# Macaron block on one core: the last feed-forward's tokens turned by VectorE and DMAs instead of TensorE

## The chip, the core and the metric

The kernel runs on one core of a Trainium2 chip. The metric is the device time of one execution in microseconds (us). A core has five engines that run side by side, each with its own instruction stream in order: TensorE (PE in the profile, with its weight loads as PEld), VectorE (DVE), ScalarE (ACT), GpSimd (POOL) and SyncE (SP, which here issues DMAs). They wait for each other by semaphores.

## The reference

The input is 16 sequences of 256 tokens with 256 features, all float32. The block is two half-weighted feed-forwards around an attention:

```python
x = x + 0.5 * ffn(layernorm(x), w1, b1, w2, b2)
x = x + attn(layernorm(x), Wq, Wk, Wv, Wo)      # 16 heads, rotary, causal
x = x + 0.5 * ffn(layernorm(x), w1, b1, w2, b2)

def ffn(x, w1, b1, w2, b2):                     # 256 -> 1024 -> 256
    h = gelu(x @ ternary(w1).T + b1)
    return h @ ternary(w2).T + b2
```

`ternary` rounds the weights to -1, 0 and 1 by a threshold. The layer norm has no gain and no bias.

## The kernel before

All 4096 tokens stay in SBUF, as eight tiles `xs[i]` of 128 partitions x 4 x 256 (a block of 512 tokens: `BT = 4` tiles of 128 tokens). The kernel runs the first feed-forward (`ffn(0, ...)`), the attention sequence by sequence (`slot`), and the last feed-forward (`ffn(2, store)`), with some overlap where they meet.

A feed-forward is a loop of steps `u`; a step has a block `i` and an eighth `f` of the 1024 hidden features. `up(i, f)` multiplies the transposed, normalized tokens `xnT[i]` with 128 columns of `w1q` into a PSUM tile named `m` (two buffers). `xnT` has two parts, a rounded `high` and the `rest`, both float32r, so that `up` is four matmuls of 128x512. ACT then computes the gelu twice from PSUM, once rounded (`h_high`) and once in full (`h_whole`), and the difference of both, `h_rest`, is made on DVE, or on POOL for f = 1, 3 and 5. `down(i, f)` runs `LATE = 2` steps later and adds the products with `w2q` into a PSUM tile `w`: eight matmuls of 128x256, alternating between `h_high` and `h_rest`. After the eighth, two DVE instructions add half the result to `xs[i]`, and `store` issues two DMAs of 256 KB on SP.

The next block's input is prepared on the way. In `step`, at f = 4 to 7 DVE computes the statistics of block i + 2 (`stats`: `st`, `mv`), and POOL makes `rstd` from them (`finish_stats`: `var`, then a power). At f = 3 `prepare(i + 1)` lets DVE normalize the four token tiles into `xn` (one buffer). At f = 5 and 6 `turn_in(i + 1, k)` turns one half of the features: PE transposes four 128x128 pieces into a PSUM tile `mm`, ACT copies them to `high`, and DVE subtracts to get `rest`. At f = 6 `add_bias(i)` adds the output bias on POOL.

The order on each engine is the order of the program for everything that is issued through the `InOrder` wrappers `tensor`, `vector`, `scalar`, `gpsimd` and `sync`. The stores go through the plain `nc.sync`, and the scheduler places them. Almost every instruction has the wrapper's line (L196) in the profile, so it is told apart by the names of its tiles.

Of the kernel before, what the change touches and what calls it, by code (L numbers as in the profile page):

```python
# [8 lines left out]
FP = mybir.dt.float32  # L9
FR = mybir.dt.float32r  # L10
BF = mybir.dt.bfloat16
AF = mybir.ActivationFunctionType
ALU = mybir.AluOpType
# [3 lines left out]
P = 128  # L17
D = 256
KC = D // P
FF = 1024  # L20
NFC = FF // P
# [9 lines left out]
def kernel(  # L31
# [17 lines left out]
    BT = 4  # L49
    TB = BT * P  # L50
    NBLK = NT // TB
# [3 lines left out]
    small = ctx.enter_context(tc.tile_pool(name="small", bufs=4))  # L55
    fp = ctx.enter_context(tc.tile_pool(name="ffn", bufs=2))
# [19 lines left out]
    b1_sb = const.tile([P, NFC], FP, name="b1_sb")  # L76
    b2_sb = const.tile([P, D], FP, name="b2_sb")
    cos_sb = const.tile([P, 2, HD], FP, name="cos_sb")
    sin_sb = const.tile([P, 2, HD], FP, name="sin_sb")
    xs = [state.tile([P, BT, D], FP, name=f"x_{i}") for i in range(NBLK)]  # L80

    flat1, flat2 = (state.tile([P, 2 * FF], FP, name=f"w_{n}") for n in range(2))
# [19 lines left out]
    for k in range(KC):  # L102
        rows = slice(k * P, (k + 1) * P)
        nc.sync.dma_start(out=wv[:, k, :], in_=wqkvT[rows, 2 * D :])
        for at in range(0, 2 * D, 4 * HD):
            n, j, e = at // D, at // P % 2, at // (4 * HD) % 2
            nc.sync.dma_start(
                out=wqk[:, k, n, j, :, e, :],
                in_=wqkvT[rows, at : at + 4 * HD].rearrange("p (r d) -> p r d", d=HD),
            )  # L110
    for at in range(0, P, HD):
        r, n = at // 32, at // HD % 2
        nc.sync.dma_start(
            out=wo[at : at + HD, :, :],
            in_=woT.rearrange("(k n r d) f -> n r d k f", n=2, r=4, d=HD)[n, r],
# [19 lines left out]
        out=mask_k,  # L135
        in_=mask_k,
# [10 lines left out]
        out=mask_b,  # L147
        in_=mask_b,
# [9 lines left out]
        out=ident_b,  # L158
        in_=ident_b,
# [25 lines left out]
    mv = [state.tile([P, NTILE, 2], FP, name=f"mv_{i}") for i in range(3)]  # L185
    rstd = [state.tile([P, NTILE], FP, name=f"rstd_{i}") for i in range(3)]
# [17 lines left out]
    def tokens(n):  # L204
        return xs[n // BT][:, n % BT, :]

    def stats(ln, n):
        st = small.tile([P, 6], FP, name="st")
        vector.bn_stats(st, tokens(n))
        vector.bn_aggr(mv[ln][:, n, :], st)  # L210

    def finish_stats(ln, first, n):

        var = small.tile([P, BT], FP, name="var")
        gpsimd.tensor_scalar(
            var[:, 0:n], mv[ln][:, first : first + n, 1], LN_EPS, 1.0, ALU.add, ALU.mult
        )
        gpsimd.tensor_tensor(
            rstd[ln][:, first : first + n], var[:, 0:n], power[:, 0:n], ALU.pow
        )  # L220
# [78 lines left out]

    LATE = 2  # L300

    def ffn(ln, after):
        xn, xnT, hT, ys = {}, {}, {}, {}

        def measure(i):
            if ln == 0:
                for t in range(BT):
                    stats(0, i * BT + t)
                finish_stats(0, i * BT, BT)

        def prepare(i, engine=None):
            xn[i] = fp.tile([P, BT, D], FP, name="xn", bufs=1)
            for t in range(BT):
                normalize(ln, i * BT + t, xn[i][:, t, :], engine)
            xnT[i] = [fp.tile([P, KC, TB], FR, name=f"xnT_{n}") for n in range(2)]

        def add_bias(i):
            gpsimd.tensor_add(xs[i], xs[i], b2_sb.unsqueeze(1).to_broadcast([P, BT, D]))

        def turn_in(i, k):  # L320
            tp = ps_mm.tile([P, TB], FP, name="mm")
            for t in range(BT):
                tensor.transpose(
                    tp[:, t * P : (t + 1) * P], xn[i][:, t, k * P : (k + 1) * P], ident
                )
            high, rest = (xnT[i][n][:, k, :] for n in range(2))
            scalar.copy(high, tp)
            return lambda: vector.tensor_sub(rest, tp, high.bitcast(FP))

        first = {}  # L330

        def up_first(i, f, to=None):
            h = first[i, f] = ps_m.tile([P, TB], FP, name="m") if to is None else to
            for n in range(2):
                for k in range(KC):
                    tensor.matmul(
                        h,
                        w1q[:, k, f * P : (f + 1) * P],
                        xnT[i][n][:, k, :],
                        start=(n == 0 and k == 0),  # L340
                        stop=(n == 1 and k == KC - 1),
                    )

        def up(i, f):
            if (i, f) not in first:
                up_first(i, f)
            h = first.pop((i, f))
            high = fp.tile([P, TB], FR, name="h_high", bufs=LATE + 3)
            rest = fp.tile([P, TB], FR, name="h_rest", bufs=LATE + 3)
            whole = fp.tile([P, TB], FP, name="h_whole", bufs=3)  # L350
            scalar.activation(high, h, AF.Gelu, bias=b1_sb[:, f : f + 1])
            scalar.activation(whole, h, AF.Gelu, bias=b1_sb[:, f : f + 1])

            engine = gpsimd if f in (1, 3, 5) and not (ln == 0 and i == NBLK - 1) else vector
            engine.tensor_sub(rest, whole, high.bitcast(FP))
            hT[i, f] = (high, rest)

        def down(i, f):
            if f == 0 and ln == 2 and i == NBLK - 1:

                ys[i] = [ps_mm.tile([P, 2, D], FP, name="mm") for t in range(0, BT, 2)]
            elif f == 0:
                y = ps_w.tile([P, BT, D], FP, name="w")
                ys[i] = [y[:, t : t + 2, :] for t in range(0, BT, 2)]
            parts = hT.pop((i, f))
            order = [(t, n) for t in range(BT) for n in range(2)]
            if ln == 2 and (i, f) == (NBLK - 1, NFC - 1):

                order = [(t, n) for n in range(2) for t in range(BT)]
            for t, n in order:  # L370

                tensor.matmul(
                    ys[i][t // 2][:, t % 2, :],
                    parts[n][:, t * P : (t + 1) * P],
                    w2q[:, f, :],
                    start=(f == 0 and n == 0 and t % 2 == 0),
                    stop=(f == NFC - 1 and n == 1 and t % 2 == 1),
                )
            if f == NFC - 1:
                for t in range(0, BT, 2):  # L380
                    xt = xs[i][:, t : t + 2, :]
                    vector.scalar_tensor_tensor(
                        xt, ys[i][t // 2], 0.5, xt, ALU.mult, ALU.add
                    )
                for t in range(0, BT, 2):
                    after(i, t)

        def begin():
            measure(0)
            if ln == 0:  # L390
                sizes(0)
            prepare(0)
            if ln == 0:
                threshold(0)
                signs(0, lambda w: w[:, :, 0 : FF // 2])
            for k in range(KC):
                turn_in(0, k)()
            if ln == 0:
                signs(0, lambda w: w[:, :, FF // 2 :])
                sizes(1)  # L400

        def step(u):
            i, f = divmod(u, NFC)
            if i < NBLK:
                up(i, f)
                if ln == 0 and u == 0:
                    threshold(1)
                if ln == 0 and u in (0, 3):
                    part = slice(0, NFC // 2) if u == 0 else slice(NFC // 2, NFC)
                    signs(1, lambda w: w[:, part, :])  # L410
                if ln == 0 and u == 4:
                    gpsimd.tensor_scalar(b2_sb, b2_sb, 0.5, 0.0, ALU.mult, ALU.add)
                if u == 1:
                    measure(1)
                if i + 1 < NBLK and (ln, i) != (2, 0):
                    if f == 3:
                        prepare(i + 1)
                    if f in (5, 6):
                        turn_in(i + 1, f - 5)()
                if f >= 4 and i + 2 < NBLK:  # L420
                    stats(ln, (i + 2) * BT + f - 4)
                    if f == NFC - 1:
                        finish_stats(ln, (i + 2) * BT, BT)
                if f == (1 if i == NBLK - 1 else 6):
                    add_bias(i)
            if u >= LATE:
                down(*divmod(u - LATE, NFC))
            if ln == 0 and u == 2 * NFC + 2:
                make_tables()
            if ln == 0 and u < (NBLK - 1) * NFC and later:  # L430
                later.pop(0)()

        return begin, step, prepare, turn_in, up_first
# [353 lines left out]
    rest = []  # L787
# [96 lines left out]
```

## Time and profile before

| | us |
|---|---|
| median of 3 runs | 600.56 (599.93 to 601.11) |
| profiled execution, its own time | 599.31 |
| its span | 597.5 |
| PE busy | 580.0 (97%) |
| DVE busy | 473.5 (79%) |
| ACT busy | 391.1 (65%) |
| POOL busy | 324.8 (54%) |

The granted TensorE clock is 1.00 of full speed over the span. The last feed-forward takes about the last 130 us: from its first steps at about 465 us to the end it has 48 transposes of `xn` on PE (272 ns each by their rows, which overlap), 24 normalizations on DVE (408 ns), 62 rounded and 62 full gelus from `m` on ACT (688 and 681 ns), and DMAs moved 1 to 59 GB/s in stretches of 20 us.

How to read the rows that follow: `out<-in` are the names of the tiles, then partitions x elements and the type; `x4` is the number of instructions that are merged into a row. The chain of work that ended last is followed back from the last instruction, at each step to what released it. Times of PE in the chain are the spacing of its instructions, since matmuls are pipelined.

### The profile page before, as it was taken

What the parts mean: (1) busy time and instruction counts of PE and PEld (TensorE: products, weight loads), DVE (VectorE), ACT (ScalarE), POOL (GpSimd) and SP (SyncE); (2) the same over time, 40 slices, a digit from 0 to 9 for tenths busy, and PEclk for the clock granted to TensorE, in tenths of its full rate; (3) what the DMA queues carried; (4) which work ended last, traced back from release to release, by engine and by line L of the source; (5) the groups of instructions that cost most, each with busy time, mean ns of one, the idle gap of its engine ahead of it and who ended that gap; (6) DMA issues with size and microseconds to landing.
All of it is one profiled execution on the core that took longest, in us unless ns stands there. A gap on an engine that the chain in (4) does not pass through costs nothing.

```text
span 597.5 us, 14414 instructions
## 1 busy us (share of the span) xinstructions
PE 580.0 (97%) x5398; PEld 467.2 (78%) x5398; DVE 473.5 (79%) x1690; ACT 391.1 (65%) x668; POOL 324.8 (54%) x301
## 2 busy tenths in 40 slices
PE   4999999999999999999999999999999999999996
PEld 3798989887777777777777777777767788888886
DVE  6877888677688999899899999999986466666743
ACT  4576666675476666766667676676765666666664
POOL 4645665693555576555855668464821454455452
PEclk9999999999999999999999999999999999999999
DMA  8810000000010011100110001100000011111101
GB/s 282 196 27 2 1 1 1 36 1 19 19 39 20 20 38 37 37 23 20 38 38 28 31 19 38 38 20 28 31 4 2 2 36 36 36 36 36 35 30 41
DMA packets 25588, 21.26 MB, mean 36 GB/s; under 512 B 11056, under 2 KB 21168, under 8 KB 25520
## 3 DMA queue, kind: packets, MB, share of 16 engines
q1 hardware_dynamic: 24960, 19.44, 10.3%
q8 instruction: 42, 0.69, 0.5%
q10 hardware_dynamic: 560, 0.92, 0.4%
q14 instruction: 26, 0.21, 0.1%
HBM read 7.51 MB, written 4.19 MB: 20 GB/s over the span
## 4 chain that ended last, share of the span: by engine, by line
PE 88%; DVE 5%; ACT 3%; issue 1%; DMA 1%; POOL 1%; DVEq 0%; SPq 0%; POOLq 0%; ACTq 0%
PE mm L196 35%; PE w L196 31%; PE m L196 23%; DMA w<-in_w1T_dram 1%; DVE xn L196 1%; ACT h_high L196 1%; DVE masked L196 1%; ACT h_whole L196 1%; DVE w2q L196 1%; DVE h_rest L196 1%; DVE w L196 1%; DVE st L196 0%; POOL h_rest L196 0%; DVE x L196 0%; ACT pT L196 0%
## 5 line engine op out<-in xcount | busy, mean ns | idle before, releaser
L196 DVE CUSTOM_DVE_ANT_0 masked<-m,mask_q 128x128 f32<-128x128 f32 x480 | 142.1, 351 | 20.6 <-PE m L196 19.7
L196 PE MATMUL m<-xnT,w1q 128*128 128x512 f32 x504 | 143.3, 405 | 0.9 <-ACT xnT L196 0.7
L196 ACT ACTIVATE pT<-w 128x768 f32<-128x768 f32 x128 | 104.1, 814 | 56.3 <-DVE w L196 55.9
L196 ACT ACTIVATE h_high<-m,b_sb 128x512 fp32r<-128x512 f32 x126 | 86.7, 688 | 79.4 <-PE m L196 79.3
L196 DVE TENSOR_TENSOR h_rest<-h_whole,h_high 128x512 fp32r<-128x512 f32 x83 | 74.7, 900 | 60.3 <-ACT h_whole L196 59.9
L196 PE MATMUL w<-w2q,h_high 128*128 128x256 f32 x480 | 120.7, 285 | 0.3 <-DVE w2q L196 0.3
L196 PE MATMUL w<-qT,kT 32*128 32x256 f32 (+1 forms) x1024 | 120.5, 348 | 0.0
L196 PE MATMUL w<-w2q,h_rest 128*128 128x256 f32 x480 | 118.0, 279 | 0.8 <-POOL h_rest L196 0.7
L196 PEld LDWEIGHTS w<-qT,kT 32*128 32x128 f32 x1024 | 90.3, 184 | 33.6 <-issue 22.8
L196 PE MATMUL m<-kT,qT 32*128 32x128 f32 x960 | 115.0, 349 | 0.3 <-ACT kT L196 0.3
L196 POOL TENSOR_TENSOR h_rest<-h_whole,h_high 128x512 fp32r<-128x512 f32 x45 | 60.1, 1335 | 85.3 <-ACT h_whole L196 85.1
L196 PEld LDWEIGHTS m<-xnT,w1q 128*128 128x128 f32 x504 | 87.4, 191 | 16.4 <-DVE xnT L196 2.9
L196 PEld LDWEIGHTS w<-w2q,h_rest 128*128 128x128 f32 x480 | 90.4, 188 | 5.9 <-POOL h_rest L196 1.2
L196 PEld LDWEIGHTS w<-w2q,h_high 128*128 128x128 f32 x480 | 90.3, 188 | 5.0 <-DVE w2q L196 0.8
L196 DVE TENSOR_TENSOR w<-w,mask_k 128x512 f32<-128x512 f32 x123 | 85.5, 695 | 3.7 <-PE w L196 3.6
L196 ACT ACTIVATE h_whole<-m,b_sb 128x512 f32<-128x512 f32 x126 | 85.8, 681 | 0.0
L196 POOL TENSOR_TENSOR o<-avs,inv 128x256 f32<-128x256 f32 x32 | 20.3, 635 | 91.6 <-DVE inv L196 91.6
L196 PE MATMUL mm<-xnT_a,wqk 128*128 128x256 f32 x256 | 68.5, 392 | 0.0
L196 PEld LDWEIGHTS m<-kT,qT 32*128 32x128 f32 x960 | 66.2, 185 | 1.5 <-ACT kT L196 0.7
L196 POOL TENSOR_TENSOR w<-w,cosT 128x512 f32<-128x512 f32 x32 | 41.3, 1289 | 27.0 <-ACT kT L196 13.4
L196 PEld LDWEIGHTS mm<-xnT_a,wqk 128*128 128x128 f32 x256 | 45.8, 189 | 10.0 <-issue 1.3
L196 POOL TENSOR_TENSOR w<-w,sinT 128x512 f32<-128x512 f32 x32 | 40.9, 1277 | 20.4 <-DMA w<-w 20.4
(92 smaller groups left out, 885.8 us busy)
## 6 DMA issues: line engine op xcount, KB each, us to landing
w<-w SPq DMA_DIRECT2D x64, 128.0 KB
out_dram<-x SPq DMA_DIRECT2D x15, 256.0 KB
x<-in_x_dram SPq DMA_DIRECT2D x7, 512.0 KB
w<-in_w2T_dram SPq DMA_DIRECT2D x1, 1024.0 KB
qT<-mT SPq DMA_DIRECT2D x64, 4.0 KB
w<-in_w1T_dram SPq DMA_DIRECT2D x1, 512.0 KB
w<-in_w1T_dram ACTq DMA_DIRECT2D x1, 512.0 KB
wqk<-in_wqkvT_dram SPq DMA_DIRECT2D x16, 32.0 KB
```

The source lines that it names most:

```text
L196: return tc.keep_in_program_order(getattr(self.engine, name)(*args, **kwargs))
```

## The change

It concerns the last feed-forward alone, and its blocks 3 to 7 (`by_blocks`). Blocks 0 to 2 are prepared as before.

- The statistics of such a block are computed at f = 2 and 3, two blocks ahead, and at f = 6 DVE makes an `offset`, minus mean times `rstd`.
- ACT normalizes the four token tiles at f = 6 and 7, as an activation with `rstd` as scale and the offset as bias.
- At f = 0 of the next block, DVE transposes the tile by blocks of 32x32 into `turned`, the second half of a weight buffer that is free by then. One DMA writes it to a DRAM tile `rows` (512 KB), and four DMAs of 128 KB bring its rows, in runs of 128 elements, into the `rest` part of `xnT`. All five are issued by SP.
- `turn_in` then only copies to `high` on ACT, and DVE subtracts in place.
- The tokens of such a block stand in another order (four groups of 32 in turn), so the gelus read and write permuted views, which puts the order right.
- The output bias of blocks 1 to 6 is added in two halves, at f = 2 and 4 instead of f = 6.

```diff
+    turned = flat2[:, FF:]
+    dram = ctx.enter_context(
+        tc.tile_pool(name="rows", bufs=2, space=bass.MemoryType.DRAM)
+    )
     def ffn(ln, after):
+        by_blocks = range(3, NBLK if ln == 2 else 0)
...
+        def offsets(i):
+            offset[i] = small.tile([P, BT], FP, name="offset", bufs=2)
+            of = slice(i * BT, (i + 1) * BT)
+            vector.scalar_tensor_tensor(
+                offset[i], mv[ln][:, of, 0], -1.0, rstd[ln][:, of], ALU.mult, ALU.mult
+            )
+        def normalize_by_blocks(i, t0, t1):
...
+                scalar.activation(
+                    xn[i][:, t, :],
+                    tokens(n),
+                    AF.Identity,
+                    bias=offset[i][:, t : t + 1],
+                    scale=rstd[ln][:, n : n + 1],
+                )
+        def turn_by_blocks(i):
+            vector.transpose(turned, xn[i].rearrange("p n (j t) -> p j n t", t=32))
+            rows = dram.tile([P, 2 * TB], FP, name="rows")
+            sync.dma_start(out=rows, in_=turned)
+            of = rows.rearrange("(a f) (k j q) -> j f k a q", a=4, k=KC, j=4)
+            xnT[i] = [fp.tile([P, KC, TB], FR, name=f"xnT_{n}") for n in range(2)]
+            for j in range(4):
+                sync.dma_start(
+                    out=xnT[i][1][32 * j : 32 * j + 32]
+                    .bitcast(FP)
+                    .rearrange("p k (a q) -> p k a q", a=4),
+                    in_=of[j],
+                )
-        def add_bias(i):
-            gpsimd.tensor_add(xs[i], xs[i], b2_sb.unsqueeze(1).to_broadcast([P, BT, D]))
+        def add_bias(i, t0=0, t1=BT):
+            xt = xs[i][:, t0:t1, :]
+            gpsimd.tensor_add(xt, xt, b2_sb.unsqueeze(1).to_broadcast([P, t1 - t0, D]))
         def turn_in(i, k):
+            if i in by_blocks:
+                high, rest = (xnT[i][n][:, k, :] for n in range(2))
+                scalar.copy(high, rest.bitcast(FP))
+                return lambda: vector.tensor_sub(rest, rest.bitcast(FP), high.bitcast(FP))
...
-            scalar.activation(high, h, AF.Gelu, bias=b1_sb[:, f : f + 1])
-            scalar.activation(whole, h, AF.Gelu, bias=b1_sb[:, f : f + 1])
+            for to in (high, whole):
+                if i in by_blocks:
+                    to = to.rearrange("p (n a t) -> p a n t", n=BT, a=4)
+                    of = h.rearrange("p (a n t) -> p a n t", n=BT, a=4)
+                else:
+                    of = h
+                scalar.activation(to, of, AF.Gelu, bias=b1_sb[:, f : f + 1])
...
         def step(u):
             i, f = divmod(u, NFC)
+            if f == 0 and i > 0 and i + 1 in by_blocks:
+                turn_by_blocks(i + 1)
...
-                    if f == 3:
+                    if f == 3 and i + 1 not in by_blocks:
                         prepare(i + 1)
                     if f in (5, 6):
                         turn_in(i + 1, f - 5)()
-                if f >= 4 and i + 2 < NBLK:
-                    stats(ln, (i + 2) * BT + f - 4)
-                    if f == NFC - 1:
-                        finish_stats(ln, (i + 2) * BT, BT)
-                if f == (1 if i == NBLK - 1 else 6):
+                if i + 2 < NBLK:
+                    early = i + 2 in by_blocks
+                    for at in {2: (0, 1), 3: (2, 3)}.get(f, ()) if early else (f - 4,):
+                        if at >= 0:
+                            stats(ln, (i + 2) * BT + at)
+                        if at == BT - 1:
+                            finish_stats(ln, (i + 2) * BT, BT)
+                    if early and f == 6:
+                        offsets(i + 2)
+                    if early and f in (6, 7):
+                        normalize_by_blocks(i + 2, 2 * (f - 6), 2 * (f - 5))
+                if ln == 2 and 0 < i < NBLK - 1:
+                    if f in (2, 4):
+                        add_bias(i, f - 2, f)
+                elif f == (1 if i == NBLK - 1 else 6):
                     add_bias(i)
```

More of the change, by code (lines that the diff above doesn't have):

```diff
@@ L315, in prepare @@
             xnT[i] = [fp.tile([P, KC, TB], FR, name=f"xnT_{n}") for n in range(2)]
-        def add_bias(i):
-            gpsimd.tensor_add(xs[i], xs[i], b2_sb.unsqueeze(1).to_broadcast([P, BT, D]))
+        offset = {}
+        def offsets(i):
[5 more added lines that the diff above has]
+        def normalize_by_blocks(i, t0, t1):
+            if t0 == 0:
+                xn[i] = fp.tile([P, BT, D], FP, name="xn", bufs=1)
+            for t in range(t0, t1):
+                n = i * BT + t
+                scalar.activation(
[21 more added lines that the diff above has]
+            gpsimd.tensor_add(xt, xt, b2_sb.unsqueeze(1).to_broadcast([P, t1 - t0, D]))
         def turn_in(i, k):
+            if i in by_blocks:
+                high, rest = (xnT[i][n][:, k, :] for n in range(2))
+                scalar.copy(high, rest.bitcast(FP))
+                return lambda: vector.tensor_sub(rest, rest.bitcast(FP), high.bitcast(FP))
             tp = ps_mm.tile([P, TB], FP, name="mm")
```

## The prediction

> **What bounds the kernel now.** I read the page first: its engine line and its summary of the chain that ended last.
>
> ```profile
> PE 580.0 (97%) x5398; PEld 467.2 (78%) x5398; DVE 473.5 (79%) x1690; ACT 391.1 (65%) x668; POOL 324.8 (54%) x301
> PE 88%; DVE 5%; ACT 3%; issue 1%; DMA 1%; POOL 1%; DVEq 0%; SPq 0%; POOLq 0%; ACTq 0%
> ```
>
> TensorE (PE) is busy and nearly always on the path. An instruction taken from it counts in full, if nothing else becomes late. Second, the chain in order of time over one block of the last feed-forward (start, duration):
>
> ```profile
> 505.62 0.44 PE mm L196 x4
> 506.06 0.94 PE w L196 x8
> 507.00 0.93 PE m L196 x4
> 507.93 0.44 PE mm L196 x4
> 508.37 0.95 PE w L196 x8
> ...
> 511.17 0.69 PE m L196 x3
> 511.86 0.02 issue
> 511.89 0.50 PE m L196
> 512.38 0.93 PE w L196 x8
> ...
> 522.15 0.94 PE w L196 x8
> ```
>
> One step f is 0.93 (`m`, four matmuls of `up`) + 0.93 (`w`, eight of `down`) = 1.87 us. A block is eight steps, 14.93, plus two groups of four transposes (`mm`, 0.44 each), plus about 0.28 at 511.17, where `up` of the new block waits for DVE's xnT. From 506.06 to 522.15 it is 16.09.
>
> Third, the timeline of the other engines there, one line each, and two ACT rows from the attention for an activation whose scale (and bias) is a column:
>
> ```profile
> 507.00 1.29 POOL L196 TENSOR_TENSOR h_rest<-h_whole,h_high 128x512 fp32r<-128x512 f32 x1 [2.43 <-ACT h_whole L196]
> 508.26 2.42 POOL L196 TENSOR_TENSOR x<-x,b_sb 128x1024 f32<-128x1024 f32 x1
> 508.55 0.68 ACT L196 ACTIVATE h_whole<-m,b_sb 128x512 f32<-128x512 f32 x1
> 509.12 0.59 ACT L196 CAST xnT<-mm 128x512 fp32r<-128x512 f32 x1
> 509.27 1.96 DVE L196 TENSOR_TENSOR h_rest<-h_whole,h_high 128x512 fp32r<-128x512 f32 x1 [0.59 <-ACT h_whole L196]
> 511.15 0.68 DVE L196 TENSOR_TENSOR xnT<-mm,xnT 128x512 fp32r<-128x512 f32 x1
> 267.94 0.50 ACT L196 ACTIVATE qT<-w,own 128x256 f32<-128x256 f32 x1
> 268.34 0.59 ACT L196 ACTIVATE kT<-w,one,own 128x256 f32<-128x256 f32 x1
> ```
>
> To be seen: ACT does two gelus per step (0.59 + 0.68 = 1.27 of 1.87 us). DVE's h_rest at 509.27 takes 1.96 instead of 0.69, because POOL's bias addition runs until 510.68: the two engines exclude each other where DVE reads two SBUF tensors.
>
> **What leaves PE.** In the changed program's instruction order, eight transposes are gone from each of the five blocks 2 to 6 (preparing blocks 3 to 7). Each of these blocks falls from 16.09 to 14.93 if nothing is late: 5 x 1.16 = 5.8 us gained. Four DVE normalizations per block (0.34 us apart) go too; DVE waits for work there, so they count nothing.
>
> **What is added, with its cover.** Per block: on DVE one transposition of 128x1024 (rows: 128x512 in 0.71, 128x256 in 0.44, so 1.08 ns per column, 1.26 us) and one small offset (nearest rows 0.18 to 0.25; I take 0.2); on ACT four normalizations (start to start 0.40 to 0.59 by the two rows above; I take 0.47); on SP five transfers. The ACT copy of xnT stays at 0.59. Statistics move from f 4 to 7 to f 2 and 3: the same DVE work, sooner. The gelus' permuted writes count nothing: ACT's `vals` copy, written in runs of 16, took 0.37, as did the contiguous `mT` copy of the same size. If strided writes cost 0.05 after all, a step has 0.6 us free on ACT.
>
> **ACT: the new wait.** Let t = 0 at a block's first `up`. In step f = 6 ACT has, in this order: two gelus, the copy k = 1, the first two normalizations, and only then the gelus of f = 7. The normalizations need the offset, which on DVE stands behind the subtraction that needs this copy. `up` 6 ends at 6 x 1.87 + 0.93 = 12.1. ACT starts 0.2 later (503.60 to 503.80 in the trace), its second gelu ends at 13.6, the copy at 14.1, the subtraction (0.69) at 14.8, the offset at 15.0. ACT waited 0.9 for that. Two normalizations take it to 16.0. Gelu 7, due at 14.2, is 1.8 late; its second half ends at 17.3. Queued behind it: `up` of the next block's f = 1 would start at 16.8 and needs the PSUM buffer that this gelu frees (two `m` buffers). PE waits 0.55. Two more normalizations (0.94) hold gelu 0: it ends at 19.4, and `up` 2, due at 19.2, loses 0.3. Sum 0.85.
>
> To this comes the exclusion of DVE and POOL. The subtraction used to read PSUM, and such a row at 491.35 took 0.69 while POOL ran h_rest. Now it reads two SBUF tensors, as h_rest does. In f = 5 it meets POOL's second half of the bias addition and its h_rest; both DVE rows behind it shift. Bounds: 0 and 1.27 (the 1.96 row less 0.69). Most of it is absorbed while DVE would be idle; I take 0.25. ACT's wait then costs PE **1.1 us** per block, between 0.55 (normalizations at 0.40, no exclusion) and 1.8.
>
> A rule that speaks against the change stands in the Trainium skill, "SBUF — State Buffer", section "Who interferes with whom": a VectorE instruction with two SBUF inputs and a GpSimd instruction that reads SBUF block each other for the whole instruction. This trace shows it for the bias addition, but not for rstd's power of 128x4: an h_rest at 44.57 took 0.69 while that ran from 43.96 to 44.97. By the rule h_rest of f = 4 would be held by it too, until about 11.7, which is still before PE's need at 12.1: by rule or row the sum is the same.
>
> **POOL: a longer queue before h_rest 5.** The bias addition, 2.42 behind h_rest 5 before, is now two halves (1.25 each by the 128x512 rows), and var and the power come before the second. Statistics end at t = 9.6 (11.1 if the block starts late), var and power take 1.2, the half 1.25: 12.1 to 13.6; h_rest 5 adds 1.29, and 0.5 where DVE gets in first (a POOL row at 122.07 took 1.74, not 1.29, with a DVE h_rest waiting). It ends at 13.4 to 15.4. PE wants it at 14.0 to 15.0. Bounds 0 and 0.9; taken: **0.5 us** per block.
>
> **The DRAM round trip.** ACT wants the rows at t = 11.7, behind gelu 5. The turn on DVE ends at 3.3 to 4.9. The write of 512 KB: the last stores of the kernel are the nearest row: issued from 593.48, 512 KB moved from 594.35 to 595.95, the program over at 597.5, so about 3.7 to landing. SP then has the two stores of the block before, done earlier (evictions end about 6.1). Four reads: issues 0.5 apart, first data 0.9 to 1.2 after issue, 0.4 of moving, 0.45 to the consumer (the `w` pair: last data 267.25, POOL starts 267.68): 3.5. Landed at 3.3 + 7.2 = 10.5 to 12.1, with ACT's need at 11.7 to 12.7 by then. Hidden, by 0.6 to 1.2 us. If that cover is gone, each us late is a us on PE, since gelu 6 stands behind the copy. Reads of 512 bytes do not occur before; bound 0 to 2 us more.
>
> **Sum.** Five blocks (1 to 5 normalize ahead; block 1 pays without gaining, block 6 gains with the last wait behind it): 5 x (1.1 + 0.5) = 8.0 lost, 5.8 gained: +2.2. The profiled execution took 599.31 (span 597.5 and 1.8 around it), so 601.5 by it; the median of the runs shown, 600.56, is 1.25 above it, so **602.8 us**.
>
> **Rivals.**
> 1. *ACT catches up, faster.* Against: the order on ACT and DVE is fixed. For: h_rest's slack of 1.5 us on DVE, and a shorter offset or activations. With a wait of 0.55 and no POOL term: 5 x 0.55 - 5.8 = -3.05, **597.5**. It decides where the two waits together stay below 1.16 per block.
> 2. *The rows land late, much slower.* Against: 7.2 us against 8.4 at hand. For: two dependent transfers, a DRAM write, small rows. 2 us later leaves about 1.2 uncovered in five blocks: 6.0 on top of 2.2, **608.8**. It decides from 0.6 to 1.2 us later than estimated.
> 3. *Waits and gain cancel*, at 1.16 per block: **600.6**.
> That the transposes stay on PE is excluded by the instruction order.
>
> **How the numbers follow.** The likeliest case, waits of 1.4 to 2.2 per block (0.2% is 1.2 us, about what a measurement of this kernel can tell from no change; 5 x 1.4 - 5.8 = +1.2), has 0.46 and its own range 601.8 to 605.8. Rival 1 has 0.24, rival 2 0.18, rival 3 0.12. Faster 0.24, same 0.12, slower 0.64. The range goes from 597.3 (just past rival 1's value; beyond it the best, all 5.8 kept, 594.8) to 608.0 (most of rival 2). Some 0.2 is left out.
>
> **What would show it.** Right: in the last stage PE has no `mm<-ident,xn` from block 3 on; xn on ACT waits for DVE's offset about 1 us per block; PE's `m` waits for ACT h_whole at a block's second step, 0.5 to 1 us, and its `w` for POOL h_rest; blocks last 16.4 to 16.7. Wrong: blocks of 15 to 15.6 without these waits (rival 1); or ACT's xnT copy waiting for a DMA (rival 2).

## The result, and the profile after

The changed kernel is slower by half a per cent: 602.75 us against 599.93 us for the kernel before on the same chip (medians of 7 runs each; ratio 1.005, 95% interval 1.0036 to 1.0065). The profiled execution took 603.67 us, its span 602.1. From the page of the changed kernel, the line of the engines and the summary of the chain that ended last:

```profile
PE 578.7 (96%) x5358; PEld 465.5 (77%) x5358; DVE 479.1 (80%) x1680; ACT 400.0 (66%) x688; POOL 326.8 (54%) x307
PE 84%; DVE 6%; ACT 5%; issue 2%; DMA 1%; POOL 1%; DVEq 0%; SPq 0%; POOLq 0%; ACTq 0%
```

PE has 40 instructions fewer, as the change has it, but it holds 84% of the chain instead of 88%: DVE and ACT have come onto it. The span grew by 4.6 us, of which 3.1 lie in the last stage (134.13 us before, 137.28 after, from the ACT table load ahead of the last feed-forward to the end). The other 1.4 were there before the changed part begins, where the two programs do the same; they are taken as the difference of two executions, since this table load lies anywhere from 462.8 to 465.1 us in the traces of this study. I measure a block by the distance of the same instruction from one block to the next: 16.09 us before, 16.80 in three of the changed blocks one after the other, of which eight steps of 1.87 to 1.875 us make 15.0. So 1.16 us left each block (two groups of transposes at 0.44 and the 0.28 that `m` had waited for xnT), and 1.8 us of waits came. What PE and ACT waited for in the last stage (total us, times, the longest):

```profile
PEld w L196 <- POOL h_rest L196: 5.1, 6, 1.4
PEld m L196 <- ACT h_whole L196: 3.7, 8, 0.7
ACT xn L196 <- DVE offset L196: 9.2, 5, 1.9
```

The kernel before has the first of these once (0.5 us), the other two not at all. The weight loads (PEld) show the whole wait; the matmul rows themselves show less of it (3.3 us for `w`, 2.1 for `m`), because their modelled ends reach over a part. Now the timeline of the block around 510 us, in which the waits arise (start, duration; in brackets the idle time ahead of the row and what ended it):

```profile
509.58 1.31 POOL L196 TENSOR_TENSOR x<-x,b_sb 128x512 f32<-128x512 f32 x1
510.15 1.29 DVE L196 TENSOR_TENSOR xnT<-xnT,xnT 128x512 fp32r<-128x512 f32 x1 [1.70 <-ACT xnT L196]
...
510.83 1.76 POOL L196 TENSOR_TENSOR h_rest<-h_whole,h_high 128x512 fp32r<-128x512 f32 x1
...
511.52 1.62 DVE L196 TENSOR_TENSOR h_rest<-h_whole,h_high 128x512 fp32r<-128x512 f32 x1
512.64 0.39 PE L196 MATMUL w<-w2q,h_rest 128*128 128x256 f32 x1 [0.47 <-POOL h_rest L196]
513.06 0.68 DVE L196 TENSOR_TENSOR xnT<-xnT,xnT 128x512 fp32r<-128x512 f32 x1
513.66 0.15 DVE L196 SCALAR_TENSOR_TENSOR offset<-mv,rstd 128x4 f32<-128x4 f32 x1
513.84 1.09 ACT L196 ACTIVATE xn<-x,offset,rstd 128x256 f32<-128x256 f32 x2 [1.85 <-DVE offset L196]
...
516.14 1.20 PE L196 MATMUL m<-xnT,w1q 128*128 128x512 f32 x4 [0.53 <-ACT h_whole L196]
```

To be seen: from 509.58 on, POOL and DVE work in turn. Their rows overlap, which I read as waiting: they end one after the other, at 510.89, 511.44, 512.59 and 513.14, and the first of them, POOL's bias half, takes 1.31, hardly more than elsewhere (1.29). The second half of the bias addition holds DVE's subtraction (1.29 instead of 0.69); this holds POOL's h_rest of f = 5 (1.76 instead of 1.29), for which PE's `w` waits; that holds DVE's h_rest of f = 6 (1.62 instead of 0.69), and the second subtraction and the offset come behind it. ACT waits 1.85 us for the offset, with the gelu of f = 7 queued behind, and PE's `m` waits for that gelu.

### The profile page after: what moved, and what is told of

Same layout as the page of the kernel before. It is cut to its first block, busy times and chain, and to the rows that moved or that the text cites. A ratio compares the mean times of both kernels' runs of the same rounds, so it can differ in the third digit from the quotient of the medians.

```text
span 602.1 us, 14468 instructions
## 1 busy us (share of the span) xinstructions
PE 578.7 (96%) x5358; PEld 465.5 (77%) x5358; DVE 479.1 (80%) x1680; ACT 400.0 (66%) x688; POOL 326.8 (54%) x307
## 4 chain that ended last, share of the span: by engine, by line
PE 84%; DVE 6%; ACT 5%; issue 2%; DMA 1%; POOL 1%; DVEq 0%; SPq 0%; POOLq 0%; ACTq 0%
PE mm L196 34%; PE w L196 29%; PE m L196 22%; ACT h_high L196 2%; ACT h_whole L196 1%; DMA w<-in_w1T_dram 1%; DVE h_rest L196 1%; DVE xn L196 1%; DVE masked L196 1%; ACT xn L196 1%; POOL h_rest L196 1%; DVE w2q L196 1%; DVE w L196 1%; DVE xnT L196 0%; DVE st L196 0%
## 5 line engine op out<-in xcount | busy, mean ns | idle before, releaser
L196 DVE TENSOR_TENSOR h_rest<-h_whole,h_high 128x512 fp32r<-128x512 f32 x83 | 76.8, 927 | 59.8 <-ACT h_whole L196 59.1
L196 PE MATMUL w<-w2q,h_rest 128*128 128x256 f32 x480 | 119.5, 282 | 3.7 <-POOL h_rest L196 3.6
L196 POOL TENSOR_TENSOR h_rest<-h_whole,h_high 128x512 fp32r<-128x512 f32 x45 | 62.1, 1380 | 96.9 <-ACT h_whole L196 88.8
```

The lines of the kernel that those rows point to most:

```text
L196: return tc.keep_in_program_order(getattr(self.engine, name)(*args, **kwargs))
```

## The experiments

The theory: the 1.16 us per block are there to be had, the added work itself is free, and the change loses by two waits, ACT's for the offset and PE's for a late POOL h_rest, both lengthened by the exclusion of DVE and POOL. Rival A: ACT's four normalizations cost by their work. Rival B: the way through DRAM costs. Each kernel ran in 5 rounds against the kernel before, on the same chip within a group (medians of before: 600.61 us for the first four runs, 600.08 for the next four, 600.27 for the last four).

| kernel | median us | ratio to before (95%) | block us |
|---|---|---|---|
| the change | 602.75 | 1.0050 (1.0036 to 1.0065) | 16.80 |
| offset early | 597.32 | 0.9954 (0.9941 to 0.9968) | 15.55 |
| bias halves at f = 0 | 612.22 | 1.0200 (1.0176 to 1.0223) | 17.98, 19.25 in turn |
| offset early, bias at f = 0 | 603.51 | 1.0053 (1.0039 to 1.0066) | 16.55 |
| before, no transposes | 602.06 | 1.0023 (1.0010 to 1.0036) | 16.55 |
| offset early, bias at f = 2 | 594.43 | 0.9909 (0.9894 to 0.9925) | 15.03 |
| before, no transposes, bias at f = 2 | 594.95 | 0.9914 (0.9898 to 0.9929) | 14.93 |
| before, bias at f = 2 | 600.22 | 0.9996 (0.9983 to 1.0010) | 16.05 |
| VectorE normalizes | 596.91 | 0.9951 (0.9936 to 0.9965) | 15.42 |
| bias at f = 2 | 599.72 | 0.9991 (0.9982 to 1.0000) | 15.95 |
| plain read | 603.06 | 1.0050 (1.0036 to 1.0063) | 16.78 |
| second hop | 620.99 | 1.0348 (1.0335 to 1.0361) | 20.2 |
| VectorE normalizes, bias at f = 2 | 594.28 | 0.9900 (0.9886 to 0.9915) | 14.93 |

### The offset ahead of the subtractions

The changed kernel, with one call moved:

```diff
+                if f == 5 and i + 2 in by_blocks:
+                    offsets(i + 2)
                 if i + 1 < NBLK and (ln, i) != (2, 0):
...
                     if f in (5, 6):
                         turn_in(i + 1, f - 5)()
...
-                    if early and f == 6:
-                        offsets(i + 2)
```

> The changed kernel, with the offset of block i + 2 made on DVE at f = 5, ahead of the two subtractions, and not behind them at f = 6. Theory (the waits, not the work, eat the gain): ACT's wait for the offset (9.2 us in five blocks of the changed kernel) goes, PE's waits for ACT h_whole (about 0.95 us per block there) go with it, the waits for POOL h_rest stay: 2 to 4.5 us under the changed kernel, so 0.5 to 1.5 us on either side of the kernel before. Rival A (ACT has simply too much work at f = 6 and 7: its four normalizations are 2 us): at most 1 us under the changed kernel. Rival B (the transfers by way of DRAM disturb the rest): no difference to the changed kernel.

Measured: 597.32 us, faster than both kernels. ACT no longer waits for the offset, and PE's `m` for no gelu. One wait is left, here on the timeline:

```profile
540.29 1.83 POOL L196 TENSOR_TENSOR h_rest<-h_whole,h_high 128x512 fp32r<-128x512 f32 x1
...
542.17 0.19 PEld L196 LDWEIGHTS w<-w2q,h_rest 128*128 128x128 f32 x1 [0.59 <-POOL h_rest L196]
```

POOL's chain ahead of it (the power 1.55 us, the bias half 1.30, h_rest 1.83) still ends too late. So the wait for the offset is the larger cost. That ACT's work is unchanged in this run and the time falls below the kernel before speaks against rival A.

### The bias addition at f = 0

```diff
-                    if f in (2, 4):
-                        add_bias(i, f - 2, f)
+                    if f == 0:
+                        add_bias(i, 0, 2)
+                        add_bias(i, 2, 4)
```

> The changed kernel, with both halves of the bias of blocks 1 to 6 added at f = 0, where POOL has nothing else, and not at f = 2 and 4. Theory: POOL's h_rest of f = 5 comes on time, PE's waits for it (about 0.8 us per block, 1.2 in block 1) go, and DVE's subtractions are held less, so that the offset and with it ACT come up to 0.8 us earlier: 3 to 6 us under the changed kernel. Rivals A and B: at most 1 us under it.

Measured: 612.22 us, 2% slower than before, and by far worse than the change. I had looked at POOL's own queue alone. The timeline of this kernel:

```profile
533.07 3.43 POOL L196 TENSOR_TENSOR x<-x,b_sb 128x512 f32<-128x512 f32 x2
533.65 1.71 DVE L196 TENSOR_TENSOR h_rest<-h_whole,h_high 128x512 fp32r<-128x512 f32 x1
535.29 1.75 DVE L196 TENSOR_TENSOR xnT<-xnT,xnT 128x512 fp32r<-128x512 f32 x1
...
537.10 0.50 PE L196 MATMUL m<-xnT,w1q 128*128 128x512 f32 x1 [1.27 <-DVE xnT L196]
```

The two halves wait for nothing, so POOL does not start them at f = 0 of their block's turn in the program but straight behind h_rest 5, in the last steps of the block before. There they hold DVE's h_rest 6 and its second subtraction, each by about 1 us, and PE waits for xnT.

That is not the whole price. The granted clock of TensorE fell too: it was 0.54 from 520 to 522 us and 0.60 in the two us after, and as low around 491 and 559 us. The two steady blocks with such a stretch last 19.25 us, the two without it 17.98. At 1.3 us for each of the three stretches, that is by estimate some 4 of the 9.5 us by which this kernel is slower than the change.

> Both edits, the early offset and the bias at f = 0. Theory: no wait longer than 0.3 us per block is left on PE, a block lasts 15.0 to 15.4 us: 5 to 8 us under the changed kernel, and 2.5 to 5 us under the kernel before. Rival A: ACT is still late by about 1 us after f = 7, so that PE waits 0.5 to 0.9 us per block and the time is that of the kernel before, within 1.2 us. Rival B: no more than 1 us under the changed kernel.

This kernel has both edits above. Measured: 603.51 us, no better than the change. The offset's wait was gone, but PE waited for DVE's xnT as in the run before (6.8 us in four blocks by the weight loads); here the clock stayed at 1.00 around these waits. An instruction's place in the program is not its time: on an engine without waits it runs ahead to wherever the engine is free.

### The kernel before without its transposes

In blocks 3 to 7 nothing is turned: the copy and the subtraction read the normalized tokens from SBUF as they are, so these blocks are computed from the wrong rows.

```diff
         def turn_in(i, k):
+            if ln == 2 and i >= 3:
+                high, rest = (xnT[i][n][:, k, :] for n in range(2))
+                of = xn[i][:, 2 * k : 2 * k + 2, :].rearrange("p n d -> p (n d)")
+                scalar.copy(high, of)
+                return lambda: vector.tensor_sub(rest, of, high.bitcast(FP))
```

> The kernel before, with the transposes of blocks 3 to 7 left out and nothing in their place: ACT copies and DVE subtracts the normalized tokens as they lie in SBUF, so the part of the computation that turns the tokens of these blocks is left out. It measures the gain alone. Theory: 1.16 us per block, 5.8 us under the kernel before, less what DVE's subtraction loses to POOL's bias addition at f = 6 now that it reads two SBUF tensors: 4 to 5.8 us under. Rival (PE was not what bounds these blocks): under 2 us.

Measured: 602.06 us, no gain but a small loss: the surprise of this study. The transposes are gone, no work is put in their place, and a block still takes 16.55 us. The timeline shows why:

```profile
525.78 2.88 POOL L196 TENSOR_TENSOR x<-x,b_sb 128x1024 f32<-128x1024 f32 x1
...
526.85 2.35 DVE L196 TENSOR_TENSOR h_rest<-h_whole,h_high 128x512 fp32r<-128x512 f32 x1
...
529.13 0.68 DVE L196 TENSOR_TENSOR xnT<-xn,xnT 128x512 fp32r<-128x512 f32 x1
...
529.86 0.50 PE L196 MATMUL m<-xnT,w1q 128*128 128x512 f32 x1 [1.34 <-DVE xnT L196]
```

The bias addition of 1024 columns holds h_rest (2.35 instead of 0.69), the second subtraction comes behind it, and PE, earlier by the transposes it no longer does, waits. Before the change the transposes were the cover of this chain. That a block is even 0.46 longer than before comes from the experiment itself: the subtractions now read two SBUF tensors instead of PSUM, the first one (1.38 instead of 0.69) gets in ahead of the bias addition, and this takes 2.88 us instead of 2.42.

### The bias addition at f = 2

The edit of the halves as above, with f = 2 in place of f = 0 (in the kernels made from the one before, the addition is split into halves for it), in three kernels: the changed one with the offset early, the one without transposes, and the kernel before as it is.

> The changed kernel with the offset issued at f = 5 ahead of the two subtractions (as in the first experiment) and, besides, both halves of the bias addition at f = 2, POOL's place behind h_rest 1 and ahead of h_rest 3, instead of f = 2 and 4. Theory (the change loses by two waits of its own, ACT for the offset and POOL late with h_rest 5; its work itself is free): the second half no longer stands ahead of h_rest 5, so PE's wait of w for POOL h_rest, about 0.6 of 15.55 us in the first experiment's steady block, goes too; a block lasts 15.0 to 15.2, and the time is 2 to 3 us below the first experiment's 597.3: 594.5 to 596. If the two halves instead hold DVE's h_rest 2 and 4 (exclusion), as the halves at f = 0 held h_rest 6, PE waits for DVE h_rest, and the time is 597 to 600. Rival A (ACT's four normalizations are the cost): ACT's work is unchanged, so no gain over 597.3. Rival B (DMA): unchanged too, 597.3.

> The kernel before with the transposes of blocks 3 to 7 left out, their copies and subtractions reading xn from SBUF instead (so these blocks are computed from rows that were not turned), and the bias addition of blocks 1 to 6 in two halves at f = 2 instead of whole at f = 6. Theory (the gain of 1.16 us per block by the transposes exists, but only once POOL's bias addition no longer holds DVE's h_rest and subtractions around the block's end): the wait of PE's m for DVE xnT of 1.4 to 1.8 us per block that was seen without the transposes alone goes; 594.8 to 596.5. Rival (PE cannot go below about 16 us per block for another reason, so taking the transposes away gains nothing in any arrangement): 599 to 602.

> The control: the kernel before, transposes and all, with the bias addition of blocks 1 to 6 in two halves at f = 2. Theory: before, PE waited 0.28 us per block for DVE's xnT, because the bias addition held h_rest; this can go at most, 6 x 0.28 = 1.7: 598.9 to 600.6. A gain as large as that of the run without transposes (4 to 6 us) would mean that the place of the bias addition alone is what matters, and the transposes do not.

Measured: 594.43, 594.95 and 600.22 us, all three as the theory had it. Set side by side with the runs above, the kernel before gains nothing by the other place of the bias addition (600.2), loses a little by the missing transposes alone (602.1), and gains 5.2 us by both. In the control the wait of `m` for xnT (0.28 us per block) is gone, and a wait of the transposes for xn (1.1 us in six) stands in its place. The first of the three, which computes everything, is as fast as the kernel that only leaves the transposes out, so ACT's normalizations, DVE's transposition and the DMAs cost nothing there that the times can tell (blocks of 15.03 us against 14.93; ACT's copy waited for the rows in one block of five, 0.3 us). Of PE's waits in its last stage this one is the largest; it stands once, as before the change:

```profile
PEld w L196 <- POOL h_rest L196: 0.5, 1, 0.5
```

> The changed kernel with both halves of the bias addition at f = 2, the offset left where the change has it, behind the subtractions of f = 6: the fourth corner beside the change (602.75), the offset early alone (597.3) and both (594.4). Theory (two separate waits): the wait for POOL h_rest goes, the wait of ACT for the offset stays, or is smaller because no bias addition is left to hold DVE at f = 5; if the two simply add, 602.75 - 2.9 = 599.9; if half of the offset's lateness came from POOL's work at f = 4 and 5, 597 to 599. Rival A (ACT's work): 602.75, no gain.

The fourth corner, the change with nothing but the bias addition at f = 2: 599.72 us. By the ratios, times 600, against the change: the offset early alone is worth 5.8 us, the bias addition alone 3.5, both 8.5. Each difference is uncertain by some 1.2 us, so the two prices add, or nearly. The edit is not the price of POOL's wait alone, though: it shortens ACT's wait for the offset as well, from 9.2 us in five blocks to this (0.93 to 0.95 in the steady blocks, where it was 1.84 to 1.88):

```profile
ACT xn L196 <- DVE offset L196: 5.1, 5, 1.3
```

Since PE is no longer held by POOL there, it pays what is left of ACT's wait in full: the steady block is 15.95 us, 0.92 more than with the offset early as well.

### VectorE normalizes

```diff
-                scalar.activation(
-                    xn[i][:, t, :],
...
-                )
+                normalize(ln, n, xn[i][:, t, :])
...
-                    if early and f == 6:
-                        offsets(i + 2)
```

> The changed kernel with VectorE instead of ScalarE normalizing, at the same places (f = 6 and 7, one tensor_scalar each), and no offset. Theory (ACT's wait for the offset and what is queued behind it is the larger of the two waits): ACT's gelus come on time, DVE does four more instructions of about 0.34 us in order, no one waits for an offset; 597 to 599.5, about as the first experiment, with the wait of w for POOL h_rest left. Rival A (ACT's work, not its wait, is the cost): the four activations of 0.5 us are gone as well, so the gain would be larger than the first experiment's 597.3, below 596. Rival (DVE is the tight engine at the block's end): the four normalizations push h_rest 7 and 0 back, 600 to 604.

> Both remedies in another form: VectorE normalizing at f = 6 and 7 without an offset (596.9 alone) and both bias halves at f = 2. Theory (nothing but the two waits is lost, and the work added is hidden on either engine): the wait for POOL h_rest of about 0.5 us per block goes here too, blocks of 14.95 to 15.1, 594 to 595.5, the same as the offset early with the bias at f = 2 (594.4). If the four normalizations on DVE hold h_rest 7 or the next block's rows once POOL's order is changed: 596 to 598.

Measured: 596.91 us, and 594.28 with both bias halves at f = 2. Within their intervals these are the two runs with the offset early (597.32 and 594.43). Taking all of ACT's new work away gains no more than taking its wait away: rival A falls. The last of these is, together with the run that has the offset early and the bias at f = 2, the fastest kernel of the study, 0.9900 of the time before (0.9886 to 0.9915); the times can't tell the two apart.

### The way through DRAM

First the reads in the order of the write, in rows of 4 KB, which leaves out the regrouping (blocks 3 to 7 are computed from other numbers); then one more copy from DRAM to DRAM ahead of the reads.

```diff
-            for j in range(4):
-                sync.dma_start(
...
-                )
+            sync.dma_start(
+                out=xnT[i][1].bitcast(FP), in_=rows.rearrange("p (k q) -> p k q", k=KC)
+            )
```

```diff
-            sync.dma_start(out=rows, in_=turned)
+            first = dram.tile([P, 2 * TB], FP, name="first")
+            sync.dma_start(out=first, in_=turned)
+            sync.dma_start(out=rows, in_=first)
```

> The changed kernel with the four reads of 512-byte rows replaced by one read of the same 512 KB in the order in which it was written (4 KB at a time), so that the rows are not regrouped and blocks 3 to 7 are computed from other numbers. Theory (the round trip through DRAM is hidden behind the steps f = 0 to 5): no difference to the change, 602.2 to 603.5. Rival B (the DMA's latency, or its traffic with small rows, costs time somewhere): faster by 1 us or more, below 601.8.

> The changed kernel with the tokens copied once more from DRAM to DRAM between the write and the four reads; nothing else changes. By the trace of the change a hop of this kind (issue, move, landing) takes some 2.8 us and the rows are there 0.5 to 0.9 us before ScalarE wants them. Theory (hidden, with that margin): ScalarE's copy now waits for a DMA in blocks 2 to 6, 1.9 to 2.5 us each, and PE with it: 5 x 1.4 to 2.5 = 7 to 12 us more, 609.5 to 615. If the margin was larger than it looked (over 3 us): 602.2 to 603.5.

Measured: 603.06 us for the plain read, the time of the change: the reads in small rows cost nothing. The plain read still goes through DRAM; that the trip as a whole costs nothing in the change is to be seen from ACT's copies, none of which waits for a DMA there, and from the run with the offset early and the bias at f = 2, which is as fast as the one with neither transposes nor these DMAs. So rival B falls. The second hop cost 18 us, more than expected. On its timeline and in its table by windows (PE, PEld, DVE, ACT and POOL busy, then the granted clock):

```profile
528.94 2.56 SPq L196 DMA_DIRECT2D xnT<-rows  x4
533.96 0.62 ACT L196 CAST xnT<-xnT 128x512 fp32r<-128x512 f32 x1 [4.14 <-DMA xnT<-rows]
535.80 2.03 PE L196 MATMUL m<-xnT,w1q 128*128 128x512 f32 x4 [2.30 <-ACT h_whole L196]
```

```profile
528.00:532.00 4.00, 4.00 (x27) 3.59 (x26) 0.68 (x2) 1.27 (x2) 3.77 (x4) 1.00 0.24 71
537.60:539.40 1.80, 1.80 (x9) 1.61 (x7) 0.00 (x0) 1.80 (x5) 0.00 (x0) 0.50 0.00 0
```

The reads took 5.0 us from the first issue to ACT's copy (5.0 to 5.1 in four of the five blocks, 5.7 in one). In the change ACT takes the copy 5.1 to 5.3 us after that issue, without waiting: if the reads take 5.0 to 5.1 us there as well, the margin is 0.1 to 0.3 us, not the 0.5 to 0.9 that I had read off the bandwidth. The hop itself took 4.05 us from issue to the next issue (4.05 to 4.7), not 2.8. And PE pays more than it waits: after 2.3 us without work the granted clock fell to 0.50.

## Why the prediction was right

It said 602.8 us by five waits of 1.6 us against a gain of 5.8; measured are 602.75 and, per term:

- **The gain, 5.8.** With both waits taken out, the change is 0.0091 below before, 5.5 us; without the transposes alone in the same arrangement it is 5.2. The size is right. What the prediction did not see is the condition: with the bias addition where it was, the gain is not there at all. The change moved that addition for its own reasons and so made the gain possible; I had counted the move as a cost only.
- **ACT's wait for the offset, 1.1 per block (0.55 to 1.8).** Four steady blocks price it: 16.80 us in the change, 15.55 with the offset early, 15.95 with the bias at f = 2, 15.03 with both. Without POOL's wait, ACT's costs 0.92 per block (15.95 less 15.03), and ACT waits 0.93 to 0.95 there: the 0.9 that the prediction had without exclusion, and a price it put at 0.85. The exclusion, put at 0.25 on PE, is what is left of the 1.77 in all: 0.33. The way there was partly wrong. The offset was to be ready 15.0 us into the block; ACT began at 15.9 and had waited 1.85, so the exclusion took about 0.9 on DVE, since four instructions in a row met, not one. It did not cost PE that much because PE had by then been held by POOL, and needed the gelu later.
- **POOL's late h_rest, 0.5 per block (0 to 0.9).** Alone it costs 0.52 (15.55 less 15.03). The case "0.5 where DVE gets in first" came in each of the steady blocks: 1.73 to 1.76 instead of 1.29. All terms together are 1.77 per steady block, against 1.6.
- **The sum.** 5 x 1.6 - 5.8 = +2.2; the medians give 2.8 and the last stage of the traces 3.1. That the median was met to 0.05 us is luck: the prediction added its 2.2 to 600.56, the median of three runs, while the median of seven is 599.93, and this 0.6 makes up for the 0.6 by which the increase was put too low.
- **The blocks.** 16.4 to 16.7 was said, 16.80 measured in the steady ones. From the gelu of f = 4 to that of the next block, the first changed block, which was to pay without gaining, grew by 1.2 us; the last, which gains without a normalization behind it, fell by 1.1.
- **What was free.** DVE's transposition took 1.245 us (1.26 predicted), two normalizations 1.09 (0.94), the offset 0.15 in four blocks and 0.62 in the first (0.2). The permuted gelus took 0.69 and 0.68, as before.
- **The round trip.** Hidden, as said, but by some 0.1 to 0.3 us instead of 0.6 to 1.2: the write was done 2.8 us after its issue instead of 3.7, the four reads (measured with the second hop) 5.0 instead of 3.5. Two errors against each other, and so partly luck. Rival 2 was nearer than its 0.18 tells; the second hop shows what it costs, 3.4 us per block.
- **Rival 1** was right about its condition. Where the two waits together stay under 1.16 us per block, the change is faster: the run with the offset early waits about 0.5 and takes 597.3. That this is nearly the rival's 597.5 is chance, since the wait left there is POOL's, and the rival had only ACT's.
- **The rule on exclusion** in the Trainium skill, "SBUF — State Buffer", "Who interferes with whom", that of two such instructions the first to start blocks the other for its whole length, fits the chain from 509.58 to 513.7 us (1.29, 1.76 and 1.62 us instead of 0.69, 1.29 and 0.69); the reading that the sum would be the same with and without it was too narrow, since it looked at one pair alone. The 1.76 row there began 0.06 us before the row ahead of it ended, with DVE's subtraction already waiting, and lost its turn to it.

What stays open: with both bias halves at f = 2 ACT waits 0.93 to 0.95 us for the offset instead of 1.85, so the 0.9 on top comes from POOL's second bias half and the h_rest 5 behind it; how it divides between these two is not shown. The steady blocks show an overlap of the two edits (1.25 and 0.85 us alone, 1.77 together), but each is read from one execution, and the medians can't confirm it.

## What to carry to other kernels

Work taken off the busiest engine pays only if the chain that runs beside it is short enough: find who ends last once it is gone, for it may have been the removed work that covered them. Where DVE and POOL share work on SBUF, cost a stretch as one queue of both engines' instructions and place the ones without waits by when their engine is free, not by their place in the program. A small instruction that another engine waits for, such as the offset here, goes in as soon as its inputs are there, ahead of long ones that can wait.

## What the runs showed of the hardware

- **A short stall can halve PE's clock for some time.** In the run with the second hop PE waited 2.3 to 2.7 us in four blocks, and the clock fell in each; in the fifth it waited 2.0 us, and the clock stayed at 1.00. In the block shown, from about 1.5 us after PE began again the granted clock was 0.50 (537.6 to 539.4 us), the eight `w` matmuls came 0.21 us apart instead of 0.12, and only after 541 us was it 1.00 again. That is 1.5 us lost on top of the stall (half of 1.8 us, and 0.4 of the next 1.6 at a clock of 0.60). The length of a single wait does not decide alone: in the run with the bias at f = 0, waits of 1.27 and 0.90 us, with 1.45 us of work between them, lowered the clock in two blocks of four, and a wait of 1.74 us near 489 us lowered it in this run and not in the one with the offset early besides. The waits of the change itself, 0.5 us at a time, left the clock at 1.00. The Trainium skill, "TensorE: Matmul & The Clock Gate", Part 1 (the clock gate), gives an idle window of about 3.4 us before the clock halves; here gaps of 2.3 us and less were enough.
- **DVE goes in ahead of POOL's next instruction.** Where DVE waits with two SBUF inputs, POOL's following instruction lengthens by some 0.45 to 0.55 us (from 1.29 to between 1.72 and 1.83), even if POOL's two follow each other without a gap.
- **Dependent transfers through DRAM.** From the issue of the 512 KB write to the issue of the reads behind it passed 2.8 us; from SBUF in runs of 4 KB. A copy of the same size from DRAM to DRAM took 4.05 to 4.7. Four reads of 128 KB in runs of 512 bytes took 5.0 to 5.1 us, once 5.7, from the first issue to the instruction that waited for them; 2.6 of these, once 3.1, were the four issues.
